# An instruction planner that counts dependent operations in full, and q and k of both halves in one block: four chained image layers on one Trainium2 core

## The chip, the cores and the metric

The kernel runs on one core of one Trainium2 chip. The metric is the time of one execution on the device in microseconds (us), smaller is better. Three runs of the kernel before gave 2657.24, 2658.87 and 2659.5 us; the median is 2658.87 us. Everything is computed in 32-bit floats.

## The reference, cut to what matters

The input x has 16 samples of 256 channels and 32 x 32 = 1024 pixels. Four layers follow each other, each on all samples:

```
# layer 0: group norm (8 groups), then attention with C = 256
x = x + proj(softmax(q(gn(x))^T k(gn(x)) / 16) v(gn(x)))
# layer 1: a gate per pixel
w1 = mean over channels; w2 = max over channels
w3 = relu(conv3x3([w1, w2])); g = sigmoid(conv3x3(w1 + w2 + w3))
x = x * g
# layer 2: group norm and attention again, with other weights
# layer 3: attention with 32-channel q and k
q = Wq x + bq; k = Wk x + bk; v = Wv x + bv
attn = softmax(clip(q^T k / sqrt(32), -10, 10))
x = gamma * (v attn^T) + x
```

## The kernel before, in words

**Weights.** `fast_path` (L498) first multiplies weight matrices together (`fold`, L600, for layers 0 and 2; `fold3`, L703, for layer 3), so that in a sample one product with m stands for q and k, and one with wvp for v and the projection. A fold is a generator in seven pieces: transposes of a weight (L610) with a copy out of PSUM (L616), products of two weights (L622) with a copy, small products with the biases (L647, L671). For layer 2 the copies are VectorE's, for layer 0 ScalarE's.

**Samples.** `sample` (L1279) runs the four layers of one sample. An attention (`attend`, L1217) makes t (tb, ta, tc, tf tiles), the values v (`values`, L1194), and for each half of 512 pixels the logits (`logits`, L921: sb, sa, sc, sf tiles), their exponentials on ScalarE, and the weighted sum (`weighted`, L978: b, af, c tiles). Each matrix product is cut in 2 x 2 blocks and done with seven block products in place of eight (`seven`, L882); the sums of blocks that this needs are VectorE's. The gate (`gate_of`, L455) puts channel means and maxima into 32-row tiles, does a first convolution as two products with a banded matrix (L466, 32 columns of the array wide), a few VectorE and ScalarE steps, and a second convolution (L478, full width). Between layers a sample goes through DRAM to change its layout, half by half (`send`, L815: four DMAs out, L821, and one back, L825). `clipped_attend` (L1347) is layer 3: `qk_products` (L1355) makes q and k of one half with products that are 64 columns wide, two side by side in the array; `qk_copies` (L1371) moves them out of PSUM with three ScalarE and three VectorE instructions for a half; `combine` (L1187) makes the four sums of blocks for the values. The last sample has a version of its own (`ending`, L1416), in which q and k of both halves already are one block.

**Order of the work.** Two streams of samples (even and odd, `stream`, L1737) are generators; each `yield` hands over to the other stream, so that products of two samples alternate. The first stream runs 30 steps alone (`OFFSET`). A third generator, `later` (L1727), runs beside the streams at the beginning and holds the rest of the preparation: the head of sample 1 (`head`, L1260: loads and group norm), the fold of layer 2, `fold3`, the banded matrices of the gate (`build_toep`, L380) and `checks` (L1158), whose `moderate` (L1105) squares a folded matrix on VectorE (L1118), pauses four steps and sums it with a product (L1132). Constants such as W_GATE1 = 1 (steps of waiting between the gate's first and second convolution) and W_SEND2 = 7 (between the last weighted sum of layer 2 and layer 3) set how many steps of the other stream lie between two steps of a sample.

**The planner.** TensorE (PE in the profile) runs its products in the order in which the program makes them. The order on VectorE (DVE), ScalarE (ACT), GpSimd (POOL) and of the DMAs on SyncE (SP) is planned when the program is built: `Plan.run` (L222) simulates all engines with a table of costs (`durations`, L107: `issue` is when the engine can take the next instruction, `done` is when the result is there, on VectorE 157 ns later), and at each point takes the ready instruction that is needed soonest. `Plan.needed` (L316) works these due times back from the times at which the products began in the simulation before. `pin` (L331) does this three times and keeps the best. In the simulation an instruction that depends on an earlier one **of its own engine** waits for nothing (L258) other than that engine's issue time; dependences across engines wait for `done`. PSUM has eight banks, which all products share in order.

**Loads.** The first DMAs are, in program order, the first half of layer 0's weights, sample 0, the second half of the weights, and then `load_more` (L375): the vectors of gammas, betas and biases (`vec`) and the scalars (`sc`); then v_bias, sample 1, layer 2's and layer 3's weights. The planner may reorder those of SP.

Of the kernel before, what the change touches and what calls it, by code (L numbers as in the profile page):

```python
# [16 lines left out]
P = 128  # L17
# [5 lines left out]
NH = HW // HALF  # L23
# [5 lines left out]
STRIP = 32  # L29
# [13 lines left out]
ROUNDS = 3  # L43


W_PLANES, W_GATE1, W_GATE2, W_SEND1, W_NORM1, W_NORM2, W_NORM3, W_SEND2, W_EXP, W_AV, W_AV3 = 9, 1, 2, 4, 2, 10, 4, 7, 2, 2, 0

S_W1, S_W2, S_B1, S_B2, S_GAMMA, NSCAL = 0, 18, 27, 28, 29, 30

# [15 lines left out]
PE, DVE, ACT, POOL, SP = range(5)  # L65
SEEN = 44, 23, 23, 100, 60
# [29 lines left out]
class Step:  # L96

    __slots__ = (
        "ins", "engine", "issue", "done", "mode", "behind", "ahead", "tiles"
    )  # L100


# [42 lines left out]
class Plan:  # L145
# [3 lines left out]
    def __init__(self, nc, book):  # L149
        self.book, self.steps, self.users, self.queues = book, [], {}, {}  # L150
        touched, masks = {}, {}
        for ins in nc.cur_bb.bb.instructions:
            outs, reads = (
                [a.bass_ap for a in side if getattr(a, "bass_ap", None) is not None]
                for side in (ins.outs, ins.ins)
            )
            if not outs or ins.engine not in ENGINES:
                continue
            s = Step()
            s.ins, s.engine = ins, ENGINES.index(ins.engine)  # L160
            s.mode = ""
            if s.engine == PE:
                size = ins.tile_size
                s.mode = "rows" if size[0] < P else ""
                if size[1] < P:
                    s.mode = "corner" if size[1] < PH else "columns"
            s.issue, s.done = durations(s.engine, ins, outs, reads, s.mode)
            s.behind, s.ahead, s.tiles = set(), [], []
            me = len(self.steps)
            for a, writes in [(a, False) for a in reads] + [(a, True) for a in outs]:  # L170
                name = a.tensor.name
                known = name in book.tiles
                if not known and "DRAM" in str(a.tensor.space):
                    continue
                key = tuple(a.tensor.shape), a.offset, tuple(map(tuple, a.ap))
                if "DRAM" in str(a.tensor.space):
                    key = (1,) + key[0], key[1], ((0, 1),) + key[2]
                if key not in masks:
                    masks[key] = self.region(*key)
                p0, p1, mask = masks[key]  # L180
                bank = "PSUM" in str(a.tensor.space)
                if bank:
                    p0, p1, mask = 0, P, -1
                before = touched.setdefault(name, [])
                if known:
                    if name not in s.tiles:
                        s.tiles.append(name)
                    self.users.setdefault(name, []).append(me)
                kept = []
                for old in before:  # L190
                    j, wrote, q0, q1, other = old
                    if (writes or wrote or bank) and q0 < p1 and p0 < q1 and mask & other:
                        s.behind.add(j)
                        if (writes or bank) and p0 <= q0 and q1 <= p1 and not other & ~mask:
                            continue
                    kept.append(old)
                kept.append((me, writes, p0, p1, mask))
                touched[name] = kept
            s.behind.discard(me)
            for j in s.behind:  # L200
                self.steps[j].ahead.append(me)
            self.steps.append(s)
        for name, users in sorted(self.users.items(), key=lambda u: u[1][0]):
            self.queues.setdefault(book.tiles[name][0], []).append(name)
# [17 lines left out]
    def run(self, rank):  # L222


        steps, n = self.steps, len(self.steps)
        begin, end = [0.0] * n, [None] * n
        free, mode = [0.0] * 5, ""
# [26 lines left out]
        def ready(i):  # L254
            s = steps[i]
            t = 0.0
            for j in s.behind:
                if steps[j].engine != s.engine or s.engine == SP:  # L258
                    t = max(t, end[j])
            for name in s.tiles:  # L260
                if name not in placed:
                    r = room(name)
                    if r is None:
                        return None
                    t = max(t, r[0])
            return t and t + SEEN[s.engine]
# [49 lines left out]
    def needed(self, begin):  # L316


        need = [math.inf] * len(self.steps)
        for i in reversed(range(len(self.steps))):  # L320
            s = self.steps[i]
            if s.engine == PE:
                need[i] = begin[i]
                continue
            for j in s.ahead:
                other = self.steps[j].engine
                last = s.issue if other == s.engine else s.done + SEEN[other]
                need[i] = min(need[i], need[j] - last)
        return [(t, i) for i, t in enumerate(need)]

    def pin(self, tc):  # L331
# [21 lines left out]
class Const:  # L353
# [18 lines left out]
        self.toep = pool.tile([P, 2 + NG, STRIP], FP, name="toep")  # L372
        self.neg_b2 = pool.tile([P, 1], FP, name="neg_b2")

    def load_more(self, nc):  # L375
        vecs, scal = self.dram
        nc.sync.dma_start(self.vec, vecs)
        nc.sync.dma_start(self.sc, scal.to_broadcast([P, NSCAL]))

    def build_toep(self, tc, work, tidx):  # L380

# [73 lines left out]
def gate_of(nc, k, small, psum, ptag, pl, rows, nm):  # L455

    for g in range(NG):
        copy = nc.scalar.copy if g % 2 else nc.vector.tensor_copy  # L460
        copy(rows[:STRIP, :2, g * NT : (g + 1) * NT], pl[g * STRIP : (g + 1) * STRIP])
    neighbours(nc, rows[:, :2])
    c1 = psum.tile([P, HALF], FP, tag=ptag, name=f"c1_{nm}")
    for i in range(2):
        nc.tensor.matmul(
            c1[:STRIP, :STRIP], k.toep[:, i, :], rows[:, i, :], start=(i == 0), stop=(i == 1)  # L466
        )
    r1 = small.tile([STRIP, STRIP], FP, tag="r1", name=f"r1_{nm}")
    nc.vector.tensor_scalar(
        r1, c1[:STRIP, :STRIP], k.sc[:STRIP, S_B1 : S_B1 + 1], 0.0, ALU.add, ALU.max  # L470
    )
    yield None
    inner = rows[:STRIP, 2, :]
    nc.vector.tensor_tensor(inner, rows[:STRIP, 0, :], rows[:STRIP, 1, :], ALU.add)
    nc.vector.tensor_tensor(inner, inner, r1, ALU.add)
    neighbours(nc, rows[:, 2])
    c2 = psum.tile([P, HALF], FP, tag=ptag, name=f"c2_{nm}")
    nc.tensor.matmul(  # L478
        c2[:, :STRIP],
        k.toep[:, 2:, :].rearrange("p g j -> p (g j)"),  # L480
        rows[:, 2, :],
        start=True,
        stop=True,
    )
    yield None

    sg = small.tile([P, NT], FP, tag="sg", name=f"sg_{nm}")
    for g in range(NG):
        gs = slice(g * STRIP, (g + 1) * STRIP)
        nc.scalar.activation(  # L490
            sg[gs], c2[gs, g * NT : (g + 1) * NT], AF.Exp, bias=k.neg_b2[gs], scale=-1.0
        )
    nc.vector.tensor_scalar(sg, sg, 1.0, None, ALU.add)
    nc.vector.reciprocal(sg, sg)
    yield sg


def fast_path(nc, tc, k, bad, x, w_l0, w_l2, w_l3, qk_bias, v_bias, tap_idx, out):  # L498
# [7 lines left out]
    with ExitStack() as ctx:  # L506
        book = Book()
# [43 lines left out]
        for c in range(CC):  # L551
            both[c].dma_start(raw["l0"][:, c, : 2 * C], w_l0[c * P : (c + 1) * P, : 2 * C])
        loaded = {0: load_x(0, both)}
        for c in range(CC):
            both[c].dma_start(raw["l0"][:, c, 2 * C :], w_l0[c * P : (c + 1) * P, 2 * C :])
        k.load_more(nc)

        vcol = wts.tile([P, 3, CC], FP, name="vcol")
        nc.sync.dma_start(vcol, v_bias.rearrange("i (c p) -> p i c", p=P))
# [143 lines left out]
        def fold3():  # L703
# [31 lines left out]
            nc.vector.tensor_tensor(qb, ps[:, CC : CC + 1], qb, ALU.add)  # L735
            nc.vector.tensor_tensor(bcol3, ps[:, :CC], vcol[:, 2, :], ALU.add)
            nc.vector.scalar_tensor_tensor(bcol3, bcol3, gam, bcol2, ALU.mult, ALU.add)
            in_strips(bcol3, bstrip3, "l3")
            wv3 = w3[:, :, 2 * DQK :]
            nc.vector.tensor_scalar(wv3, wv3, gam, None, ALU.mult)  # L740
# [606 lines left out]
        def clipped_attend(xt, y, lane, b):  # L1347
# [320 lines left out]
                return  # L1668

            steps = values(lane, left, right_of(*folded["l3"]), f"l3_{b}")  # L1670
            for h in range(NH):
                qk_copies(h, qk_products(h))
                if h:
                    combine(left)
                yield
                if not h:
                    next(steps)
                    yield
            yield from steps
            tv = value_sums(lane)  # L1680
            yield
# [45 lines left out]
        def later():  # L1727

            in_strips(bcol0, bstrip0, "l0")
            chores[0].extend(to_tokens(tokens[0]))  # L1730
            yield from in_turn([head(1), fold("l2", 1, L2_GAMMA)])
            fold3()
            chores[1].extend(to_tokens(tokens[1]))
            yield from k.build_toep(tc, work, tidx)
            yield from checks()
# [349 lines left out]
```

## Time and profile before

| what | us |
|---|---|
| median of three runs | 2658.87 |
| the profiled execution, whole | 2656.41 |
| its span, from first to last instruction | 2654.6 |
| PE busy / DVE busy / ACT busy / POOL busy | 2629.1 / 2192.8 / 1341.7 / 72.1 |
| first product of the program starts at | 4.54 |
| two samples, one of each stream, repeat after | 324.7 |

The granted TensorE clock is 0.997 on average over the span. A product of 32-bit floats appears as two records in the trace, so that a block of eight products is "x16". The busy time of PE is made of modelled ends of pipelined products: what a group costs is read from the start of one group to the start of the next, not from the busy column. Times in a timeline are microseconds from the start of the span; in brackets stands how long the engine was idle before a group, and what ended the wait.

### The profile page before, as it was taken

How to read it: one execution, taken by the hardware profiler on the slowest of the kernel's cores; microseconds unless marked ns; L12 is line 12 of the kernel's file. 1: busy time of each engine (PE TensorE's matmuls, PEld its weight loads, DVE VectorE, ACT ScalarE, POOL GpSimd, SP SyncE). 2: the span in 40 equal slices, each digit the busy share in tenths (PEclk: the TensorE clock that was granted, in tenths of full speed). 3: DMA queues.
4: the chain of work that ended last, by engine and by line, in shares of the span. 5: the costliest groups of instructions: out<-in, count | busy, mean ns of one | idle time of the engine just before them, and what ended most of it. 6: DMA issues, size and time to landing. Idle time of an engine off the chain costs nothing.

```text
span 2654.6 us, 47938 instructions
## 1 busy us (share of the span) xinstructions
PE 2629.1 (99%) x18998; PEld 2366.1 (89%) x18998; DVE 2192.8 (83%) x4180; ACT 1341.7 (51%) x2825; POOL 72.1 (3%) x172
## 2 busy tenths in 40 slices
PE   8999999999999999999999999999999999999998
PEld 7898989988998889889899898998989989898897
DVE  7898887988879887788878888788897888878777
ACT  4454455544555455654455545555455544545443
POOL 4000000000000000000000000000000000000000
PEclk9999999999999999999999999999999999999999
DMA  4021111211111120211201212012111121101111
GB/s 117 1 64 49 50 40 25 64 49 57 33 38 51 49 74 15 57 48 45 69 9 57 62 35 65 18 47 65 48 49 33 32 64 49 49 17 33 49 39 44
DMA packets 135878, 123.08 MB, mean 46 GB/s; under 512 B 12768, under 2 KB 126688, under 8 KB 135648
## 3 DMA queue, kind: packets, MB, share of 16 engines
q1 hardware_dynamic: 133776, 118.76, 16.0%
q8 instruction: 153, 2.51, 0.4%
q10 hardware_dynamic: 1872, 1.18, 0.1%
q14 instruction: 77, 0.63, 0.1%
HBM read 69.58 MB, written 50.33 MB: 45 GB/s over the span
## 4 chain that ended last, share of the span: by engine, by line
PE 97%; DVE 2%; ACT 0%; DMA 0%; issue 0%; DVEq 0%; ACTq 0%
PE b_l L862 19%; PE c_l L862 13%; PE af_l L862 13%; PE sb_l L862 13%; PE sc_l L862 8%; PE vb_l L862 5%; PE sf_l L862 4%; PE sa_l L862 4%; PE vc_l L862 3%; PE tb_l L862 3%; PE s L1386 3%; PE tc_l L862 2%; PE vf_l L862 2%; PE va_l L862 2%; PE qk L1360 1%; PE tf_l L862 1%
## 5 line engine op out<-in xcount | busy, mean ns | idle before, releaser
L862 PE MATMUL sb_l<-t_l,x 128*128 128x256 f32 x1024 | 255.3, 381 | 0.0
L862 PE MATMUL b_l<-vt,e_l 128*128 128x128 f32 x2048 | 250.1, 275 | 0.0
L862 PEld LDWEIGHTS b_l<-vt,e_l 128*128 128x128 f32 x2048 | 242.6, 192 | 4.9 <-issue 2.3
L973 ACT ACTIVATE e_l<-e_l 128x512 f32<-128x512 f32 x256 | 159.0, 630 | 130.0 <-DVE e_l L894 128.1
L862 PEld LDWEIGHTS sb_l<-t_l,x 128*128 128x128 f32 x1024 | 185.2, 190 | 32.0 <-issue 10.3
L963 ACT COPY e_l<-sb_l 128x512 f32<-128x512 f32 x256 | 149.6, 585 | 119.2 <-PE sb_l L862 117.8
L862 PE MATMUL c_l<-tv,cb_l 128*128 128x129 f32 x1504 | 185.8, 276 | 0.0
L894 DVE TENSOR_TENSOR e_l<-sc_l,e_l 128x512 f32<-128x512 f32 x128 | 87.8, 686 | 116.2 <-PE sc_l L862 87.7
L862 PEld LDWEIGHTS c_l<-tv,cb_l 128*128 128x128 f32 x1504 | 176.5, 191 | 6.8 <-PE qk L1360 3.1
L975 ACT ACTIVATE e_l<-e_l 128x1024 f32<-128x1024 f32 x128 | 135.3, 1057 | 91.7 <-DVE e_l L894 91.5
L894 DVE TENSOR_TENSOR e_l<-sb_l,e_l 128x512 f32<-128x512 f32 x256 | 164.2, 681 | 4.2 <-PE sb_l L862 1.3
L1402 ACT ACTIVATE e<-s 128x512 f32<-128x512 f32 x256 | 134.8, 599 | 50.4 <-PE s L1386 49.8
L778 ACT ACTIVATE xr<-xr,bstrip 128x128 f32<-128x128 f32 (+1 forms) x376 | 140.4, 437 | 25.5 <-DVE xr L785 13.9
L862 PE MATMUL sc_l<-tc_l,xs_l 128*128 128x256 f32 x512 | 133.0, 382 | 0.0
L862 PE MATMUL sf_l<-tc_l,x 128*128 128x256 f32 x512 | 132.5, 382 | 0.0
L862 PE MATMUL sc_l<-t_l,xs_l 128*128 128x256 f32 x512 | 132.2, 381 | 0.0
L862 PE MATMUL sb_l<-tc_l,xs_l 128*128 128x256 f32 x512 | 131.4, 379 | 0.0
L862 PE MATMUL sa_l<-t_l,x 128*128 128x256 f32 x512 | 131.4, 379 | 0.0
L862 PE MATMUL af_l<-tv,e_l 128*128 128x128 f32 x1024 | 125.7, 275 | 0.0
L862 PE MATMUL c_l<-vt,e_l 128*128 128x129 f32 x1024 | 125.7, 275 | 0.0
L862 PE MATMUL af_l<-vt,e_l 128*128 128x128 f32 x1024 | 125.5, 276 | 0.0
L862 PE MATMUL b_l<-tv,e_l 128*128 128x128 f32 x1024 | 125.4, 275 | 0.0
(304 smaller groups left out, 5835.5 us busy)
## 6 DMA issues: line engine op xcount, KB each, us to landing
x<-mid_x SPq DMA_DIRECT2D x64, 512.0 KB, 3.5
xr<-in_x_dram SPq DMA_DIRECT2D x64, 256.0 KB, 4.9
mid_x<-t_z SPq DMA_DIRECT2D x128, 128.0 KB, 2.3
mid_x<-t_l SPq DMA_DIRECT2D x128, 128.0 KB, 2.3
x<-in_x_dram SPq DMA_DIRECT2D x62, 256.0 KB, 4.0
out_dram<-xr SPq DMA_DIRECT2D x124, 128.0 KB, 2.3
raw_l<-in_w_l_dram SPq DMA_DIRECT2D x1, 1024.0 KB, 7.3
raw_l<-in_w_l_dram SPq DMA_DIRECT2D x2, 256.0 KB, 4.0
```

Source lines behind the costliest of these rows:

```text
L778: nc.scalar.activation(y[:, s, ts], y[:, s, ts], AF.Identity, bias=bias[:, s : s + 1])
L862: mm = nc.tensor.matmul(out, left, right, start=fresh and m == 0 and (lone or i == 0), stop=(m == len(pairs) - 1), skip_group_check=True,)
L894: nc.vector.tensor_tensor(dst, src, dst, ALU.add)
L963: nc.scalar.copy(block(i, j), ps.rearrange("p (m n) -> p m n", m=2))
L973: nc.scalar.activation(part, part, AF.Exp)
L975: nc.scalar.activation(e[:, m : m + 2, :], e[:, m : m + 2, :], AF.Exp)
L1360: nc.tensor.matmul(ps[i * PH : (i + 1) * PH, : qt * P].rearrange("p (g n) -> p g n", g=qt), w3qk[:, c, i], xt[:, g0 : g0 + qt, c], start=( ...
L1386: nc.tensor.matmul(ss[g][:, j * 2 * P : (j + 1) * 2 * P].rearrange("p (t g j) -> p t g j", t=TPH, g=2), qk[gs, mh, 1 - blk, j * P : (j + 1 ...
L1402: nc.scalar.activation(by_strip[:, :, :, qa], ss[g].rearrange("p (m t n) -> p m t n", m=2, t=TPH), AF.Exp,)
```

## The change

Nothing is computed differently. Six edits:

1. `Plan.run`: an instruction waits for `done` of all that it depends on, of its own engine too; only product after product on PE is left out. `Plan.needed` counts `done` and the hand-over in the same way.
2. Loads of inputs get due times that keep them in program order on their queue.
3. `load_more` is cut in two: the vectors are loaded behind sample 0 and ahead of the second half of layer 0's weights; the scalars stay behind these.
4. The gate's first convolution loads all 128 columns of the array (a window of the banded matrices; the extra outputs aren't read), and W_GATE1 is 2.
5. `fold3` hands over twice between the bias of layer 3 and its move into strips.
6. Layer 3 of samples 0 to 14 first does the first two block products of the values, then q and k of both halves as one block with all twelve copies and `combine`; before, q and k of the first half came ahead of these products and those of the second half behind them. A sample has one step less there, and one more in its gate.

```diff
-W_PLANES, W_GATE1, W_GATE2, W_SEND1, W_NORM1, W_NORM2, W_NORM3, W_SEND2, W_EXP, W_AV, W_AV3 = 9, 1, 2, 4, 2, 10, 4, 7, 2, 2, 0
+W_PLANES, W_GATE1, W_GATE2, W_SEND1, W_NORM1, W_NORM2, W_NORM3, W_SEND2, W_EXP, W_AV, W_AV3 = 9, 2, 2, 4, 2, 10, 4, 7, 2, 2, 0
...
-                if steps[j].engine != s.engine or s.engine == SP:
+                if not steps[j].engine == s.engine == PE:
                     t = max(t, end[j])
...
+            s.load = ins.opcode == "DMACopy" and all(
+                "DRAM" in str(a.tensor.space) and a.tensor.name not in book.tiles for a in reads
+            )
...
+            if s.load:
+                need[i] = loads.get(s.engine, math.inf)
             for j in s.ahead:
-                other = self.steps[j].engine
-                last = s.issue if other == s.engine else s.done + SEEN[other]
-                need[i] = min(need[i], need[j] - last)
+                need[i] = min(need[i], need[j] - s.done - SEEN[self.steps[j].engine])
+            if s.load:
+                loads[s.engine] = need[i]
...
+    wide = k.toep.rearrange("p g j -> p (g j)")
     for i in range(2):
         nc.tensor.matmul(
-            c1[:STRIP, :STRIP], k.toep[:, i, :], rows[:, i, :], start=(i == 0), stop=(i == 1)
+            c1[:, :STRIP],
+            wide[:, i * STRIP : i * STRIP + P],
+            rows[:, i, :],
+            start=(i == 0),
+            stop=(i == 1),
         )
...
         loaded = {0: load_x(0, both)}
+        k.load_vectors(nc)
         for c in range(CC):
             both[c].dma_start(raw["l0"][:, c, 2 * C :], w_l0[c * P : (c + 1) * P, 2 * C :])
-        k.load_more(nc)
+        k.load_scalars(nc)
...
             nc.vector.scalar_tensor_tensor(bcol3, bcol3, gam, bcol2, ALU.mult, ALU.add)
+            yield
+            yield
             in_strips(bcol3, bstrip3, "l3")
...
-            for h in range(NH):
-                qk_copies(h, qk_products(h))
-                if h:
-                    combine(left)
-                yield
-                if not h:
-                    next(steps)
-                    yield
+            next(steps)
+            yield
+            for h, ps in enumerate([qk_products(h) for h in range(NH)]):
+                qk_copies(h, ps)
+            combine(left)
+            yield
             yield from steps
...
-            fold3()
+            yield from fold3()
```

More of the change, by code (lines that the diff above doesn't have):

```diff
@@ L98 @@
     __slots__ = (
-        "ins", "engine", "issue", "done", "mode", "behind", "ahead", "tiles"
+        "ins", "engine", "issue", "done", "mode", "behind", "ahead", "tiles", "load"
     )
@@ L319, in needed @@
         need = [math.inf] * len(self.steps)
+        loads = {}
         for i in reversed(range(len(self.steps))):
@@ L373, in __init__, with load_vectors, load_scalars @@
         self.neg_b2 = pool.tile([P, 1], FP, name="neg_b2")
[L375 to L378, printed above, removed]
+    def load_vectors(self, nc):
+        nc.sync.dma_start(self.vec, self.dram[0])
+    def load_scalars(self, nc):
+        nc.sync.dma_start(self.sc, self.dram[1].to_broadcast([P, NSCAL]))
     def build_toep(self, tc, work, tidx):
```

## The prediction

> **What bounds the kernel now.** I read the page's busy line first, then PE's waits, then PE's timeline at the places that change, then VectorE's order ahead of the two long waits.
>
> ```profile
> PE 2629.1 (99%) x18998; PEld 2366.1 (89%) x18998; DVE 2192.8 (83%) x4180; ACT 1341.7 (51%) x2825; POOL 72.1 (3%) x172
> ```
>
> PE is busy for 99% of the span: only work taken off PE, or PE's idle time, can shorten the run. PE's waits say where it idles:
>
> ```profile
> PE reach_l L1132 <- DVE msq_l L1118: 4.7, 1, 4.7
> PE fold_l L622 <- DVE wt_l L616: 4.6, 1, 4.6
> PE wtp_l L610 <- DMA raw_l<-in_w_l_dram: 4.5, 1, 4.5
> PE vb_end L862 <- ACT vt L1436: 1.3, 1, 1.3
> PE tb_l L862 <- DVE x L439: 0.7, 1, 0.7
> ```
>
> Each occurs once: all lie in the first 77 us or in the last sample. From 100 to 2600 us PE waits for nobody, so there only the products' own cost counts. PE's timeline (start, busy, group, records) in a middle sample shows q and k of layer 3:
>
> ```profile
> 254.36 1.95 PE L862 MATMUL b_l<-vt,e_l 128*128 128x128 f32 x16
> 256.23 1.08 PE L1360 MATMUL qk<-x,w3qk 128*64 128x256 f32 x8
> 257.25 2.05 PE L862 MATMUL af_l<-tv,e_l 128*128 128x128 f32 x16
> 259.14 1.06 PE L862 MATMUL vb_l<-w,x 128*128 128x128 f32 x8
> ```
>
> The reader is to see the starts: a block of 16 full-width records takes 1.785 us from start to start where full-width work follows it (the 1.78 to 1.79 between such groups). Here two such blocks and the 64-column block take 259.14 - 254.36 = 4.78. The narrow block therefore costs 4.78 - 3.57 = 1.21 us. The gate:
>
> ```profile
> 133.67 1.95 PE L862 MATMUL af_l<-vt,e_l 128*128 128x128 f32 x16
> 135.55 0.31 PE L465 MATMUL c_l<-rows,toep 128*32 128x32 f32 x4
> 135.79 2.05 PE L862 MATMUL c_l<-tv,cb_l 128*128 128x129 f32 x16
> 137.68 0.35 PE L478 MATMUL c_l<-rows,toep 128*128 128x32 f32 x2
> ```
>
> The first convolution costs 137.68 - 133.67 - 3.57 = 0.44 us. Now the head, PE and then VectorE:
>
> ```profile
> 31.02 0.60 PE L610 MATMUL wtp_l<-ident,raw_l 128*128 128x128 f32 x4
> 36.23 3.59 PE L622 MATMUL fold_l<-raw_l,wt_l 128*128 128x256 f32 x8 [4.62 <-DVE wt_l L616]
> 39.66 1.03 PE L862 MATMUL sb_l<-t_l,x 128*128 128x256 f32 x4
> ...
> 31.73 0.16 DVE L426 SCALAR_TENSOR_TENSOR ve_l<-both_l 128x2 f32<-128x2 f32 x1
> 31.81 0.75 DVE L632 TENSOR_SCALAR m_l<-fold_l 128x256 f32<-128x256 f32 x2
> ...
> 35.03 0.81 DVE L439 TENSOR_SCALAR x<-x,a_l,bb_l 128x1024 f32<-128x1024 f32 x1
> 35.76 0.75 DVE L616 COPY wt_l<-wtp_l 128x256 f32<-128x256 f32 x2
> ```
>
> PE's transposes were done at 31.6; the copy for which PE waits ran on VectorE at 35.76, behind work for later layers (m_l) and for sample 1 (x). VectorE wasn't short of an input but had another order. The eight records behind the wait take 3.43 us from start to start, where such records take 0.215 each elsewhere (1.72): the clock had fallen, and the windows view gives 0.79 granted between 31.4 and 39.7 us.
>
> **What the Trainium skill says.** "TensorEngine Tiling (Array Packing)", Key Properties: a change of tiling mode drains TensorE. The trace agrees: 0.09 us going into the 64-column block (1.87 - 1.785) and 0.11 coming out of it (1.89 - 1.785), and some time at the change itself. "TensorE: Matmul & The Clock Gate", LDWEIGHTS: a weight load's time goes by its columns, 128/1.2 = 107 ns for the full width; full-width records here follow each other after 1.785/16 = 0.112, which fits. The same page's Part 1: an idle window halves the clock for some microseconds; the slow records behind the waits agree. "VectorE: DVE Perf Modes", The DRAIN you can't avoid: an operation doesn't start before the one ahead has left the pipe, unless it isn't held. Both kinds are in the trace: in the group norm's chain each small operation starts after the one ahead has ended (pitch 0.21 to 0.28 us), while the two independent copies of 0.41 at 35.76 together take 0.75. The old plan prices a dependent small operation at its issue, 0.09 us, so it thinks such chains shorter by 0.12 to 0.19 an operation.
>
> **The change, part by part** (sum against the profiled execution, 2656.41 us).
>
> *q and k in one block.* The last sample has it already: 16 records are busy for 1.95 us, where 8 are for 1.08, so an appended half costs 0.87. A half of its own costs 1.21. Saved 0.34 a sample, in samples 0 to 14: **-5.1 us**. All of it is on PE's path. Its six extra copies in one place (0.47 us each on ACT, 0.49 on DVE) and `combine` lie beside PE.
>
> *First convolution at full width.* Four records with a full weight load at 0.112 make 0.45, against 0.44 now; if the second convolution's price holds (139.73 - 137.68 - 1.785 = 0.265 for one product), it is 0.53. I take 0.45, as the second convolution's extra comes with a wait that ends just before it, and the first one's inputs are there 5 us ahead: 16 x 0.01 = **+0.2**, at most +1.5. A gain is excluded, since four full loads are its floor. The extra gate step costs nothing: it is the other stream's products.
>
> *Vectors and loads.* The old plan had issued `vec` second on SP (1.20 us), the weights' second half third, and sample 0 from 2.13; now sample 0 starts at 1.2 on both queues, `vec` follows near 4.2 (the two loads of sample 0 take 3.0 to issue), then the weights near 4.7. With the 3.5 to 4.0 us to landing of these two, `vec` is there at about 7.8 (first needed at 9.45, L647) and the weights at about 8.7 (needed at 10.26, L610). What is moved back behind them on SP is layer 2's weight, from 5.85 to about 10.8; 7.3 us to landing makes 18.1, needed at 18.69. Sample 0's statistics start up to 0.9 earlier than 7.58, so that the 0.70 wait of tb on x goes: **-0.5**, between -0.7 and +1.5 if a landing is late.
>
> *Plan, at the fold of layer 2.* PE has no product between the transposes and the fold, so a wait stays: an operation in progress (0.3), two copies (0.75), hand-over (0.2), in all 1.2. Gone are 3.4 of the 4.6 and the slow clock, 1.7: **-5.0**, between -6.0 and 0.
>
> *Plan and `fold3`, 44 to 50 us.* The 0.62 wait of strips on bcol goes, as two steps of stream products lie between; the products behind it run slowly (46.37 to 49.9: 1.8 us over their usual 0.215 a record)[...]. I take **-1.5**, between -2.4 and 0.
>
> *Plan, at reach.* 4.7 of waiting and 2.0 of slow clock behind it. VectorE is busy from 57 to 77 and reaches msq at 76.07. In the new plan two more steps of stream products (about 3.4 us) stand ahead, and chains are priced. I take two thirds of 6.7: **-4.5**, between -6.7 and 0.
>
> *What comes back.* VectorE is idle for only 9 us between 14.6 and 81 us (16.23 of 16.8, 8.02 of 8.3, 6.80 of 10.3, 18.20 of 22, 7.93 of 9 are busy). PE's gain of 11 there doesn't fit without putting work off (turns of sample 1, checks): I charge **+2.5**. The tail keeps its order of products: 0, plus or minus 1.
>
> Sum: -5.1 + 0.2 - 0.5 - 5.0 - 1.5 - 4.5 + 2.5 = -13.9, that is 2642.5 us for the profiled execution. The median of runs lies 2.5 above the profiled execution: **2645.0 us**.
>
> **The rivals.** *Only the blocks pay* (plan leaves the head's waits as they are, because VectorE is full there, or moves them): -5.1 + 0.2, and up to 2 from the head: 2652 to 2656, say 2654. For it: 57 of 66 us busy. Against it: the copy at 35.76 was overtaken by work with later consumers. *The plan does still better*, all three waits go and the tail shrinks: 2638. *Small new waits* in the steady part eat most of it: 2658.
>
> *Slower: the second half of layer 2's output comes too late for q and k.* PE runs in program order, so a late half stops both streams. Now the second q/k block starts 3.1 to 3.6 us after the landing of its half (twice 1.0 and 2.4). It starts 6.4 to 6.6 us after the first block; after the change only 4.5 us later than that place (1.79 for the values' products, 1.72 to 1.79 for the other stream, 0.95 for the first half's q and k). That leaves 1.1 to 1.6 us. It decides once VectorE's turns and the DMAs behind them slip by over 1.1 us: each further microsecond costs 15 us, and a slip of 3 makes 2645 + 15 x 1.8 = 2672. Against it: the planner charges the half's load with 4.6 us where the trace shows 3.2, so its due time asks for more margin than the chip needs.
>
> **How the numbers follow.** Forecast 0.60 (2640 to 2651), only blocks 0.20, still better 0.06, small new waits 0.07, late half 0.07. The range reaches from 2639 to 2655: about 0.19 is left out (most of "still better", a little of "only blocks", small waits, late half). A measurement tells 0.2%, 5.3 us, from no change: below 2653.5 is faster. This takes the forecast, "still better" and 0.12 of "only blocks": 0.78; same 0.15; slower 0.07.
>
> **What would show it.** Right: 15 blocks of 16 records on L1360 ahead of the last sample's; two samples repeat after 324.0 us, not 324.7; the wait at L622 below 1.5 us with full clock behind it; a shorter or no wait at L1132. Wrong: a wait of PE on the DMA into x at L1360 that returns with every sample (late half); PE's waits at L622 and L1132 unchanged; new waits on VectorE between 40 and 100 us as long as those that went.

## The result, and the profile after

| | us |
|---|---|
| before, median of six runs (2655.72 to 2659.50) | 2657.57 |
| after, median of six runs (2642.92 to 2648.95) | **2645.78** |
| after / before, with the 95% interval | 0.9954 (0.9942 to 0.9966) |
| profiled execution after (before: 2656.41) | 2642.92 |
| its span (before: 2654.6) | 2641.1 |
| two samples repeat after (before: 324.71) | 324.30 to 324.33 |

The forecast was 2645.0, and 2642.5 for the profiled execution. The six runs after fall into two groups, three of 2642.9 to 2643.6 us and three of 2648.0 to 2649.0 at a lower granted clock (0.996 to 0.997 against 0.999), so that their median lies where no run does. Its nearness to 2645.0 is therefore partly chance, and medians some 3 us apart are told apart here only where their intervals are. The profiled execution is the shortest of the six. The page's busy line after:

```profile
PE 2622.2 (99%) x18998; PEld 2368.0 (90%) x18998; DVE 2143.3 (81%) x4180; ACT 1349.1 (51%) x2825; POOL 69.7 (3%) x172
```

The counts on this line are the same as before to the last one; only the order and the shapes of some instructions changed. PE is still the bound. PE's waits after (total, times, longest, in us):

```profile
PE wtp_l L623 <- DMA raw_l<-in_w_l_dram: 4.8, 1, 4.8
PE tb_l L877 <- DVE x L446: 2.0, 1, 2.0
...
PE fold_l L635 <- DVE wt_l L629: 1.0, 1, 1.0
```

The wait of 4.7 on `msq` is gone, that on `wt` fell from 4.6 to 1.0, and the first one on the norm's x, 0.7 before, has become 2.0. PE's timeline of the head (start, busy, group; in brackets the idle time ahead of it):

```profile
16.08 2.08 PE L877 MATMUL tb_l<-x,m_l 128*128 128x512 f32 x2 [1.97 <-DVE x L446]
17.95 1.65 PE L877 MATMUL ta_l<-x,m_l 128*128 128x512 f32 x2
...
34.01 0.60 PE L623 MATMUL wtp_l<-ident,raw_l 128*128 128x128 f32 x4
35.58 1.99 PE L635 MATMUL fold_l<-raw_l,wt_l 128*128 128x256 f32 x8 [0.97 <-DVE wt_l L629]
37.41 1.03 PE L877 MATMUL sb_l<-t_l,x 128*128 128x256 f32 x4
...
45.78 0.41 PE L699 MATMUL strips_l<-bcol,ident 128*32 128x2 f32 x8
...
70.82 1.03 PE L1147 MATMUL reach_l<-msq_l,ones 128*128 128x256 f32 x4
```

The fold behind the copy now takes 37.41 - 35.58 = 1.83 us from start to start where it took 3.43: with the wait the slow clock went too. Strips and reach stand without a bracket, so no wait shows there.

The span of 13.5 us less divides at two products that both kernels have, sample 1's first (85.90 before, 74.71 after) and the last sample's second convolution (2452.86 and 2439.01): the head gave 11.2, the 2,364 us between them 2.66, and the tail lost 0.35.

### The profile page after: what moved, and what is told of

The parts are those of the page before. It is cut to its first block, busy times and chain, and to the rows that moved or that the text cites. A ratio compares the mean times of both kernels' runs of the same rounds, so it can differ in the third digit from the quotient of the medians.

```text
span 2641.1 us, 47888 instructions
## 1 busy us (share of the span) xinstructions
PE 2622.2 (99%) x18998; PEld 2368.0 (90%) x18998; DVE 2143.3 (81%) x4180; ACT 1349.1 (51%) x2825; POOL 69.7 (3%) x172
## 4 chain that ended last, share of the span: by engine, by line
PE 98%; DVE 1%; ACT 0%; DMA 0%; issue 0%; SPq 0%; DVEq 0%; ACTq 0%
PE b_l L877 19%; PE af_l L877 13%; PE c_l L877 13%; PE sb_l L877 13%; PE sc_l L877 8%; PE vb_l L877 5%; PE sf_l L877 4%; PE sa_l L877 4%; PE vc_l L877 3%; PE tb_l L877 3%; PE s L1401 3%; PE tc_l L877 2%; PE vf_l L877 2%; PE va_l L877 1%; PE tf_l L877 1%; PE qk L1375 1%
## 5 line engine op out<-in xcount | busy, mean ns | idle before, releaser
L877 PEld LDWEIGHTS sb_l<-t_l,x 128*128 128x128 f32 x1024 | 185.0, 190 | 31.8 <-issue 10.3
L909 DVE TENSOR_TENSOR e_l<-sb_l,e_l 128x512 f32<-128x512 f32 x256 | 172.9, 683 | 9.6 <-PE sb_l L877 5.0
L877 PEld LDWEIGHTS af_l<-vt,e_l 128*128 128x128 f32 x1024 | 119.4, 192 | 8.1 <-issue 8.1
```

The source lines that it names most:

```text
L877: mm = nc.tensor.matmul(out, left, right, start=fresh and m == 0 and (lone or i == 0), stop=(m == len(pairs) - 1), skip_group_check=True,)
L909: nc.vector.tensor_tensor(dst, src, dst, ALU.add)
```

## The experiments

The theory: the accounting of dependent operations (edit 1) removes the head's waits, the two hand-overs in `fold3` help it, the q/k block shortens every sample by 0.34, and the parts don't need each other. The rivals, one after the other: the hand-overs alone suffice; the head's gain comes from the loads; the block gains without the accounting too, or it doesn't. Medians and ratios are to the kernel before on the same chip.

### The accounting alone (p1_plan_only)

```diff
# on the kernel before
-                if steps[j].engine != s.engine or s.engine == SP:
+                if not steps[j].engine == s.engine == PE:
...
-                last = s.issue if other == s.engine else s.done + SEEN[other]
-                need[i] = min(need[i], need[j] - last)
+                need[i] = min(need[i], need[j] - s.done - SEEN[self.steps[j].engine])
```

> The kernel before with the planner's accounting of dependent operations alone (old order of loads, old gate, old q/k blocks, no yields in fold3). Theory 1 (the accounting is what emptied the head of its waits): the wait at layer 2's fold falls from 4.6 us to about 1 and its slow clock goes (-5.2), the wait at reach shrinks by at least half (-3.5 to -6.7), the steady part stays at 324.7 us for two samples: about 2648 us, 2645 to 2651. Rival (the two yields and the order of the loads did it): both waits stay, 2656 to 2658. If the late start of the first t product (16.08 in the changed kernel) is the accounting's doing and not the loads', it shows here too.

Measured: 2655.05, ratio 0.9991 (0.9984 to 0.9998). Its longest waits beside that for the weight:

```profile
PE c_l L476 <- ACT rows L450: 5.7, 8, 0.7
PE strips_l L684 <- DVE bcol L735: 1.9, 1, 1.9
PE fold_l L620 <- DVE wt_l L614: 0.9, 1, 0.9
```

The accounting alone takes away the wait at reach and all but 0.9 us of that at the fold; the wait at strips grows to 1.9. The head is 9.0 us shorter (sample 1's first product starts at 76.91, not 85.90). But the second convolution waits in every second sample (0.7 us, eight times), and two samples repeat after 325.63 us, 0.92 more than before. Most of what the head gains is given back there, and the 2645 to 2651 that was expected isn't reached. The likely reason is that with W_GATE1 = 1 the chain between the two convolutions has too little cover; no run has the accounting with W_GATE1 = 2 alone.

### The q/k block alone (p2_qk_only)

```diff
# on the kernel before: edit 6, and
-W_PLANES, W_GATE1, ... = 9, 1, ...
+W_PLANES, W_GATE1, ... = 9, 2, ...
...
+            next(steps)
+            yield
+            for h, ps in enumerate([qk_products(h) for h in range(NH)]):
+                qk_copies(h, ps)
+            combine(left)
+            yield
```

> The kernel before with q and k of both halves as one block and W_GATE1 = 2 alone (old planner, old narrow convolution, old loads). Theory 1: 15 blocks fewer at 0.346 us make -5.2, two samples repeat after 324.0 us and the head keeps its waits: about 2652.4 us. Rival (the second half comes late under the old plan, which knows nothing of the chain's length): a wait on the DMA into x returns with every sample, 2655 or more.

Measured: 2663.81, ratio 1.0025 (1.0015 to 1.0034): slower.

```profile
PE tc_l L862 <- DVE xr L1021: 2.3, 8, 0.3
PE sb_l L862 <- ACT e_l L963: 1.7, 8, 0.2
```

The head's waits at reach and at the fold are those of the kernel before (4.7 and 4.5). In the steady part the block does save its 0.347 us a sample, but waits of 0.3 and 0.2 us return with every pair of samples, on VectorE and on ScalarE; with smaller ones they must make some 1.4 us a pair. For the pair repeats after 325.4 on average, 0.7 more than before although the block saves 0.7, and eight pairs make most of the 5.6 us. The expectation that the block pays by itself falls.

### The accounting taken out again (p3_after_old_plan)

The two edits of p1_plan_only undone in the kernel after; all else stays.

> The changed kernel with the old accounting of dependent operations (loads in program order, wide first convolution, one q/k block and the yields stay). Theory 1: the wait at layer 2's fold returns (+5), the wait at reach in part (+2 to +6, as the two yields put work ahead of it), the first t product starts near 14.6 again (-3), the wait of 0.31 us in the gate of every second sample goes (-2.5): about 2649 us, 2646 to 2654. Rival (yields and loads did it): 2641 to 2645, as only the losses go.

Measured: 2657.19, ratio 0.9997 (0.9988 to 1.0005).

```profile
PE fold_l L637 <- DVE wt_l L631: 3.7, 1, 3.7
PE tc_l L879 <- DVE xr L1038: 2.3, 8, 0.3
PE sb_l L879 <- ACT e_l L980: 1.6, 8, 0.2
...
PE reach_l L1149 <- DVE msq_l L1135: 0.4, 1, 0.4
```

Without the accounting nothing of the gain is left. The median is 11.4 us above the kernel after's, and above the 2646 to 2654 that was expected. In the profiled executions, which lie 15.7 apart, 3.8 are lost in the head, 9.2 between sample 1's first product and the last second convolution (with each pair of samples 325.37 - 324.32 = 1.05, by the same waits as in p2_qk_only) and 2.7 in the tail. Reach waits little here: the two hand-overs of `fold3`, or the accounting, each take most of that wait away.

### The hand-overs of fold3: without them, and alone (p6_no_yields, p10_yields_only)

```diff
# p6_no_yields, on the kernel after (p10_yields_only: the reverse, on the kernel before)
-            yield
-            yield
             in_strips(bcol3, bstrip3, "l3")
...
-            yield from fold3()
+            fold3()
```

> The changed kernel without the two hand-overs in fold3. Theory 1 (they put products between bcol and strips): a wait of 1 to 2 us at strips returns, as in the kernel with the accounting alone (1.9), with some slow clock behind it: +2 to +3.5, about 2648.5; the streams' positions later than that stay. Rival (the accounting makes bcol early enough): within 0.7 us of 2645.8.

Measured: 2649.96, ratio 0.9973 (0.9962 to 0.9984). PE's timeline of p6_no_yields at the strips:

```profile
47.18 0.48 PE L699 MATMUL strips_l<-bcol,ident 128*32 128x2 f32 x8 [2.17 <-DVE bcol L750]
47.60 2.08 PE L875 MATMUL sf_l<-tc_l,x 128*128 128x256 f32 x4
49.47 1.68 PE L875 MATMUL sc_l<-t_l,xs_l 128*128 128x256 f32 x4
```

Without the hand-overs PE waits 2.17 us for `bcol`, and the four records behind take 49.47 - 47.60 = 1.87 us, not 0.86 (4 x 0.215): the clock has fallen. The profiled executions differ by 6.5 us in all, 3.7 of it at this place, the rest at the start, the fold and in the tail; the medians differ by 4.2.

> The kernel before with the two hand-overs in fold3 alone. Theory (at reach either of the two is enough, the accounting or the hand-overs; at the fold only the accounting helps): the wait at reach falls from 4.7 to under 1.5 with its slow clock, the 0.6 at strips goes, the wait at layer 2's fold stays at 4.6, the steady part stays at 324.7 for two samples: -6 to -9, about 2650. Rival (the accounting is needed at reach): the wait there stays at 3 or more, 2654 to 2657.

Measured: 2653.94, ratio 0.9984 (0.9977 to 0.9990).

```profile
PE fold_l L622 <- DVE wt_l L616: 3.0, 1, 3.0
PE reach_l L1134 <- DVE msq_l L1120: 1.5, 2, 1.1
```

Alone they gain 3.7 us against the same chip's 2657.60, less than the 6 to 9 expected. The waits at reach come to 1.5 in all, the longest 1.1, with 1.4 more at reachb behind it, and layer 3's strips wait no more; against that tb waits 1.5 at the start, where it was 0.7. The fold's wait drops to 3.0, but not by a better order: PE's transposes come 2.5 us later than before (33.53 against 31.02) and the copy 0.9 later (36.64 against 35.76), behind the same work. The fold needs the accounting.

### Two q/k blocks again (p11_two_blocks)

The kernel after with the old loop of `qk_products` and `qk_copies`, which is one step more in a sample.

> The changed kernel with q and k of the two halves in two blocks again, and so one step more in a sample. Theory 1: +0.347 us in 15 samples, +5.2: two samples repeat after 325.0 us, about 2651. Rival (the shifted step brings waits of its own, as it did under the old accounting): 2654 or more.

Measured: 2648.79, ratio 0.9967 (0.9956 to 0.9979). From sample 1's first product to the last second convolution it takes 2369.04 us where the kernel after takes 2364.30. That is 4.74 for 15 samples, 0.32 each, with no wait that returns. Here the interval overlaps with that of the kernel after; it is the profile that shows the block's price. The head of this execution is 3.4 us longer as well (78.10 against 74.71). Its VectorE does the same work in the same order up to the scaling of layer 3's weight `w`, but stands still for that load for 2.82 us, where the kernel after stood still for 1.15, and PE then waits 2.4 us for `xs`. So landing times alone can move the head by some microseconds.

### The gate's first convolution (p4_gate_later, b1_loads_planes, b2_loads_narrow)

In odd samples the wide convolution costs more than its four records. Two kernels give its rows a step more, one makes it narrow again; b1 and b2 stand on p9_loads_old, which is told next.

```diff
# p4_gate_later, on the kernel after
-W_PLANES, W_GATE1, W_GATE2, ... = 9, 2, 2, ...
+W_PLANES, W_GATE1, W_GATE2, ... = 10, 2, 1, ...
# b1_loads_planes, on p9_loads_old
-W_PLANES, W_GATE1, W_GATE2, ... = 9, 2, 2, ...
+W_PLANES, W_GATE1, W_GATE2, ... = 10, 2, 2, ...
# b2_loads_narrow, on p9_loads_old
-            c1[:, :STRIP], wide[:, i * STRIP : i * STRIP + P], rows[:, i, :],
+            c1[:STRIP, :STRIP], k.toep[:, i, :], rows[:, i, :],
```

> The changed kernel with W_PLANES = 10 and W_GATE2 = 1: both convolutions of the gate one step later, all else at its place. Theory 1 (the first convolution of odd samples waits 0.31 us because its rows are only just there): the step of 1.8 us covers it, -2.5 us: two samples repeat after 324.0 us and the time is about 2643.3. Rival (the planner works to due times, so the rows come a step later as well): the wait stays, 2645.8.

> The changed kernel with the loads as before (2642.4 us so far) and W_PLANES = 10, with no step taken back elsewhere, so that a sample has one step more. Theory 1: the wait of 0.31 us at the first convolution of odd samples goes (-2.5) and, unlike with W_GATE2 = 1, the second norm keeps its time: about 2640. Rival (any new position of the streams against each other can bring new waits, as in the kernels before): 2643 or more, with a wait that returns in every second sample.

> The changed kernel with the loads as before and the first convolution 32 columns wide again. Theory 1 (the 0.31 us wait is the plan's, the full width itself costs 0.011 us): even samples cost 0.437 instead of 0.448, odd ones wait for their rows as well, some 0.7 instead of 0.76: 2641.5 to 2642.5. Rival (the full width itself brings the wait): -2.5, 2639.9.

Measured: 2656.37 (0.9993, 0.9985 to 1.0002), 2651.88 (0.9980, 0.9971 to 0.9988) and 2640.68 (0.9941, 0.9926 to 0.9956). With a step more the first convolution costs 0.445 in every sample, as forecast; but the norm of layer 2 comes a step later, and PE stops there in every second sample. PE's waits of b1_loads_planes, and VectorE's timeline ahead of one of them:

```profile
PE tb_l L873 <- issue: 10.3, 8, 1.3
```

```profile
154.54 0.80 DVE L442 TENSOR_SCALAR x<-x,a_l,bb_l 128x1024 f32<-128x1024 f32 x1
```

The view puts that wait down to "issue", but the x that tb needs ended at 155.34 and tb starts at 155.45. The expectation that the extra step is free falls: 0.76 - 0.45 = 0.3 us of cover at the gate were bought with 1.3 us at the norm. p4_gate_later shows the same 10.3.

The narrow form gains 1.7 us on the median of p9_loads_old, which the intervals don't tell apart; but its pair repeats after 324.09 where it was 324.30. PE's timeline of b2_loads_narrow in an odd sample:

```profile
160.87 1.06 PE L873 MATMUL va_l<-wvp_l,x 128*128 128x128 f32 x8
161.98 0.31 PE L469 MATMUL c_l<-rows,toep 128*32 128x32 f32 x4
162.22 1.16 PE L873 MATMUL vc_l<-vc_l,xs_l 128*128 128x128 f32 x8
163.22 1.06 PE L873 MATMUL vb_l<-vc_l,xs_l 128*128 128x128 f32 x8
```

163.22 - 160.87 - 2 x 0.893 = 0.56 (0.893 is a block of eight full-width records), against 0.76 of the full width at the same place. That lies between what was expected (0.7) and the rival (0.44): the late rows cost in both forms, but 0.12 in the narrow one and 0.31 in the wide one. This kernel has the lowest median of the study, 5.1 us below that of the kernel after, yet the two ratios' intervals overlap.

### The loads, and the start (p5_x1_late, p9_loads_old, p7_lookahead)

The change made the first product of sample 0 later by 1.5 us (16.08 against 14.61). VectorE's timeline of the kernel after shows why:

```profile
11.97 0.18 DVE L425 COPY wide_l<-rmv_l 128x64 f32<-128x64 f32 x1
12.07 0.69 DVE L415 BATCH_NORM_STATS2 st_l<-x 128x6 f32<-128x512 f32 x1
12.68 0.23 DVE L427 STREAM_TRANSPOSE both_l<-wide_l 128x64 f32<-128x64 f32 x1
12.83 0.65 DVE L415 BATCH_NORM_STATS2 st_l<-x 128x6 f32<-128x512 f32 x1
13.40 0.14 DVE L433 SCALAR_TENSOR_TENSOR ve_l<-both_l 128x2 f32<-128x2 f32 x1
13.46 1.28 DVE L415 BATCH_NORM_STATS2 st_l<-x 128x6 f32<-128x512 f32 x2
...
15.43 1.19 DVE L446 TENSOR_SCALAR x<-x,a_l,bb_l 128x512 f32<-128x512 f32 x2
```

Between the small operations of sample 0's norm stand statistics of sample 1 (L415), 0.65 us each. Sample 1 is there by 13.7 us now; before, it landed between 15.2 and 18.8. And the plan now knows that a dependent chain has pauses, and fills them, with work longer than the pause. From the chain's first aggregate to x it is 4.82 us, where it was 3.49. With the accounting alone (p1_plan_only) the first product starts at 15.42, and with the loads without the accounting (p3_after_old_plan) at 15.81. Three ways to undo this:

```diff
# p5_x1_late, on the kernel after: sample 1 behind layer 2's and 3's weights
-        loaded[1] = load_x(1, (nc.sync, nc.sync))
         nc.sync.dma_start(raw["l2"], w_l2.rearrange("(c p) o -> p c o", p=P))
...
+        loaded[1] = load_x(1, (nc.sync, nc.sync))
         bcol0, bcol2, bcol3 = (...)
# p9_loads_old, on the kernel after: edits 2 and 3 undone
-            if s.load:
-                need[i] = loads.get(s.engine, math.inf)
...
-            if s.load:
-                loads[s.engine] = need[i]
...
-        k.load_vectors(nc)
         for c in range(CC):
             both[c].dma_start(raw["l0"][:, c, 2 * C :], w_l0[c * P : (c + 1) * P, 2 * C :])
+        k.load_vectors(nc)
# p7_lookahead, on the kernel after: give way to what is more urgent and nearly ready
                     i = min((rank[i], i) for u, i in times if u <= t + 1)[1]
+                    soon = [(rank[j], u, j) for u, j in times if u <= t + min(250, steps[i].issue)]
+                    if soon and min(soon)[0] < rank[i]:
+                        _, t, i = min(soon)
```

> The changed kernel with the loads of sample 1 behind the weights of layers 2 and 3 and the index table. Theory 1 (sample 0's norm was late because the plan, which now sees a pause after each dependent operation, fills the pauses with sample 1's statistics of 0.69 us, as sample 1 lands at 10.65 to 13.7 us): without sample 1 there the chain from the first aggregate to x takes about 3.5 us again instead of 4.8, the wait of tb falls from 2.0 to under 0.7 and the slow clock behind it goes: -2 to -3 us, about 2643.3. Rival (the chain is long by itself): 2645.8; and worse if sample 1's norm then comes late.

> The changed kernel with the loads as before: vectors and scalars behind the weights in program order, and no due times that keep the order of the queue. Theory 1 (the loads in program order brought sample 1 early and with it the filled pauses): sample 1 lands near 15 to 19 us as before, the first t product starts near 14.6 to 15.6, -1 to -3: about 2643.8. Rival (the order of the loads is worth what it was made for): 2646 to 2648.

> The changed kernel with one more rule in the planner: an instruction that would start gives way to one that is needed sooner and becomes ready within 0.25 us. Theory 1 (pauses in urgent chains are filled with long operations): the first t product starts before 15 us, -2 to -3; odd samples' first convolution no longer waits 0.31 us (-2.5): 2641 to 2644. Rival (giving way wastes VectorE's time, which is busy for 81%): new waits of PE in the steady part, 2648 or more.

Measured: 2642.58 (0.9939, 0.9926 to 0.9953), 2642.38 (0.9941, 0.9927 to 0.9954) and 2663.64 (1.0023, 1.0012 to 1.0034). In the first two, sample 1's statistics are gone from the chain, but the wait of tb only fell to 1.23 and 1.16, and in p5_x1_late the product still starts at 16.05. VectorE's timeline of p5_x1_late shows what took their place:

```profile
14.67 0.20 DVE L718 TENSOR_SCALAR w<-w 128x64 f32<-128x64 f32 x1 [1.33 <-DMA w<-in_w_l_dram]
```

and that of p9_loads_old, at the same place:

```profile
13.07 0.20 DVE L714 TENSOR_SCALAR w<-w 128x64 f32<-128x64 f32 x1 [1.39 <-DMA w<-in_w_l_dram]
```

The plan had layer 3's weight landed sooner than it was, and put its scaling ahead of the norm's last steps; VectorE runs in order and stood still for 1.3 to 1.4 us. The look-ahead does shorten the start (first product at 15.24), but the order that it makes costs more than it brings: PE waits 5.7 us in all at reach, and 0.6 us at tb in eight samples. That cure falls. Both load orders have medians 3.2 and 3.4 below the kernel after's, as was expected, but the intervals overlap. In the profiles the head is 1.0 us shorter in p9_loads_old (73.75 against 74.71) and no shorter in p5_x1_late (74.79), and the pairs repeat after 324.30 in both. So the load edits brought no gain, and that they cost some 3 us is not shown; p5_x1_late's median came out as expected while its start didn't.

## Why the prediction was right, point by point

| step, profiled execution | forecast | measured |
|---|---|---|
| q/k block, 15 samples | -5.1 | -5.2 |
| first convolution, with what it does to the second | +0.2 | +2.3 |
| vectors and loads (start to first transposes) | -0.5 | +3.0 |
| fold of layer 2 | -5.0 | -5.25 |
| strips and `fold3` | -1.5 | -2.2 |
| reach | -4.5 | -6.7 |
| what comes back | +2.5 | 0 |
| tail | 0 | +0.35 |
| sum | -13.9 | -13.5 |

The sum is right, but that it is so near is in part luck: the first convolution and the loads cost 5.6 us more than forecast, and the head's three waits, with the charge that didn't come, gave 5.65 more. The small rest of 0.2 between the rows and the span lies in the steady part.

**q and k in one block: right.** PE's timeline of the kernel after:

```profile
247.02 1.95 PE L877 MATMUL af_l<-tv,e_l 128*128 128x128 f32 x16
248.90 1.95 PE L1375 MATMUL qk<-x,w3qk 128*64 128x256 f32 x16
250.78 2.05 PE L877 MATMUL af_l<-vt,e_l 128*128 128x128 f32 x16
252.67 1.06 PE L877 MATMUL vc_l<-vc_l,xs_l 128*128 128x128 f32 x8
```

252.67 - 247.02 - 3.57 = 2.08, where two separate blocks cost 2 x 1.21 = 2.42: 0.34 saved. Over a pair of samples the two blocks' excess over full-width work fell from 1.390 to 0.696 us, 0.347 a sample, in every kernel with the one block. This agrees with the drain that the Trainium skill ("TensorEngine Tiling (Array Packing)", Key Properties) names for a change of tiling mode, paid once and not twice; no run here separates it from other costs of starting a block. What failed is half a sentence: that the block's copies "lie beside PE". They do so only under the new accounting; under the old one the change of layer 3 brings the waits of p2_qk_only and p3_after_old_plan. Which of the moved instructions delays `xr` and `e` there was not taken apart.

**First convolution: the size was off, by its place.** In even samples the forecast of 0.45 holds:

```profile
122.47 1.95 PE L877 MATMUL af_l<-vt,e_l 128*128 128x128 f32 x16
124.26 0.53 PE L473 MATMUL c_l<-rows,toep 128*128 128x32 f32 x4
124.62 2.03 PE L877 MATMUL c_l<-tv,cb_l 128*128 128x129 f32 x16
126.49 0.72 PE L877 MATMUL b_l<-tv,e_l 128*128 128x128 f32 x5
```

126.49 - 122.47 - 3.57 = 0.45. In odd samples it doesn't:

```profile
163.57 1.06 PE L877 MATMUL va_l<-wvp_l,x 128*128 128x128 f32 x8
164.67 0.63 PE L473 MATMUL c_l<-rows,toep 128*128 128x32 f32 x4
165.14 1.14 PE L877 MATMUL vc_l<-vc_l,xs_l 128*128 128x128 f32 x8
166.12 1.06 PE L877 MATMUL vb_l<-vc_l,xs_l 128*128 128x128 f32 x8
```

```profile
164.38 0.24 ACT L459 COPY rows<-rows 32x62 f32<-32x62 f32 x1
```

166.12 - 163.57 - 2 x 0.893 = 0.76. ScalarE's copy of the rows ends at 164.62, and the convolution starts at 164.67. The prediction's step "its inputs are there 5 us ahead" was read from the kernel before (4.5 to 4.8 in odd samples, 5.2 in even ones). With the accounting alone (p1_plan_only) 2.3 us are left in odd samples, with edit 6 under the old accounting (p2_qk_only) 0.38: the step that left layer 3 moved the gate forward and took most of the margin. Both together leave 0.05, and even samples keep 4.1. The wait is the cause: in b1_loads_planes the rows are 1.4 us ahead, and the same convolution costs 0.45. Eight times 0.31, less 0.34 that the second convolution gains in even samples, make the +2.3.

**Vectors and loads: wrong in sign.** The forecast looked at landings alone. Sample 0's last one came 0.5 us sooner (8.79), near what was worked out; the vectors landed at 9.20 and not 7.8, the second half of the weights at 9.54 and not 8.7, both still in time for 9.65 and 10.46. What it missed is in VectorE's timeline above: sample 1 now lands early enough to be put into sample 0's chain. 1.3 us of wait more, some 1.5 of slow clock behind it (17.95 - 16.08 = 1.87 us for two records of 512 columns, against 0.86), and 0.2 that this execution's first load came later (4.76 against 4.54) make the 3.0.

**Fold, strips, reach: right, and a little small.** VectorE's timeline of the kernel after at the fold:

```profile
32.33 0.80 DVE L446 TENSOR_SCALAR x<-x,a_l,bb_l 128x1024 f32<-128x1024 f32 x1
...
35.11 0.74 DVE L629 COPY wt_l<-wtp_l 128x256 f32<-128x256 f32 x2
```

PE's transposes end at 34.61, and the copy follows 0.5 us later; before, it followed 4.1 us later (31.6 and 35.76). But it starts only 0.65 us sooner than before, and sample 1's x still stands ahead of it: it is PE that comes 3.0 us later, so here the rows "vectors and loads" and "fold" share their microseconds. The lateness doesn't explain the gain: in p3_after_old_plan PE is as late (transposes at 33.55), and the copy, at 37.42, leaves it waiting 3.7 us; in p1_plan_only PE is early (32.21), the copy starts at 33.29, ahead of x, and PE waits 0.9. In b2_loads_narrow too it is 31.50 and 32.43. At the strips and at reach the wait went altogether, and the forecast had kept a third of the one at reach. p1_plan_only and p3_after_old_plan together show the cause for the fold (the accounting), p6_no_yields and p10_yields_only for the strips (the hand-overs); for reach the accounting is enough, and the hand-overs alone take most of the wait.

**What comes back: nothing.** The charge of 2.5 rested on VectorE being full there. It is: the windows view of the kernel after, for 31.4 to 39.7 us (busy time of PE, PEld, DVE, ACT, POOL; clock, DMA share, GB/s):

```profile
31.40:39.70 8.30, 7.33 (x51) 6.68 (x51) 8.30 (x20) 8.29 (x19) 7.49 (x14) 1.00 0.27 54
```

VectorE is busy for all of the 8.30 us, and for all of the 10.30 behind them, of which it worked only 6.80 before; and yet up to 100 us PE has no new wait on it. So it wasn't the amount of work that PE waited for but its order. That what was put off had consumers far behind is the likely reason.

**The rivals.** *Only the blocks pay* is refuted: the head gave 11.2 of 13.5. *The late half* didn't come: PE never waits on it. From its landing to its products it is 1.5 to 2.0 us in even samples (0.6 once) and 2.4 to 4.1 in odd ones, mostly more than the forecast's 1.1 to 1.6. *Small new waits* came in one place, the odd samples' gate, and took 2.3 us, not the 13 that this case needed. But p1_plan_only, p2_qk_only and b1_loads_planes show how near it was: one constant or one part less, and waits of 0.2 to 1.3 us return with every pair. Alone, accounting, block (with W_GATE1 = 2) and hand-overs gave -3.2, +5.6 and -3.7 us, -1.3 together; the whole change gave -11.8. The steps were added up as if they were independent, and in the steady part they are not.

## What to carry to other kernels

Where an engine is full and the bound one waits for it, look at what ran there just before the wait: if that had later consumers, a better order can be worth the whole wait and the slow clock behind it, as at the fold and at reach here, where the full engine was no reason to discount it. Where a step is taken out, or a chain's price is changed, read the margins of all inputs again, since those of the old order no longer hold: 4.8 us became 0.05. And a plan that fills pauses fills them with whatever has landed, and believes the landing times: both of the start's delays, statistics inside a chain and an operation that stood still for its DMA, come from there.

## What the runs showed of the hardware

- With the rows 0.05 us ahead in odd samples, the 32-column convolution costs 0.56 us and the full-width one 0.76; with rows that are there in time they cost 0.44 and 0.45. The narrow form may be cheaper there because the cost of its change of tiling mode passes during the wait; that reading is not tested. Full width was no gain for a product with so few records.
- The length of a wait alone doesn't tell whether slow records follow. Behind waits of 0.95 to 1.07 us at tb (p1_plan_only, p7_lookahead, p3_after_old_plan) and 1.50 at the fold (p6_no_yields) the records kept their pace. Behind 0.62 at the strips (before) and 1.16 and 1.53 us at tb (p9_loads_old, p10_yields_only) they were slow, and so they were behind 1.97 and 2.17 (after, p6_no_yields); but behind 2.49 at tb (p11_two_blocks) they weren't:

```profile
14.90 1.82 PE L873 MATMUL tb_l<-x,m_l 128*128 128x512 f32 x2 [1.16 <-DVE x L442]
16.52 1.91 PE L873 MATMUL ta_l<-x,m_l 128*128 128x512 f32 x2
```

```profile
16.87 1.12 PE L877 MATMUL tb_l<-x,m_l 128*128 128x512 f32 x2 [2.49 <-DVE x L446]
17.83 1.02 PE L877 MATMUL ta_l<-x,m_l 128*128 128x512 f32 x2
```

The first is p9_loads_old's timeline (granted clock 0.50 from 16 to 18 us), the second p11_two_blocks' (1.00 there). The Trainium skill ("TensorE: Matmul & The Clock Gate", Part 1) has the clock halved after an idle window; the 0.50 agrees, but from which length of a wait it counts the runs don't show.
